# A four-batch sequence block on one core: statistics and four pairs pinned in VectorE's order, 14 instead of 12 pairs of a causal convolution made ahead

## The chip, the cores and the metric

The kernel runs on one core of a Trainium2 chip. Five engines work side by side, each through its own queue in order: TensorE (PE; its weight loads are shown apart as PEld), VectorE (DVE), ScalarE (ACT), GpSimd (POOL) and SyncE (SP). An instruction that waits for something holds up all that stands behind it in its queue. SP and POOL also issue the DMA transfers, which run on 16 DMA engines. Matrix products go to PSUM, everything else lies in SBUF or in device memory. The metric is the device time of one execution in microseconds.

## The reference

The input is `x` of shape (4, 512, 128, 64): 4 batches, 512 time steps, and 128 x 64 = 8192 channels D. All is float32. Layer 0 is, for each batch:

```python
xn = layernorm(x)                       # over the 8192 channels
k, v, r = xn @ Wk, xn @ Wv, sigmoid(xn @ Wr)          # to 64 states
s_t = decay * s_(t-1) + k_t * v_t       # a scan over time
x = x + (r * s) @ Wo
x = x + gelu(conv(layernorm(x), freq_W) + freq_b)     # 3 taps along 128, 64 to 64 channels
to = causal_depthwise_conv(layernorm(x), time_W) + time_b   # 3 taps along time, per channel
x = x + layernorm(to)
x = x + gelu(x @ ffn_W1 + ffn_b1) @ ffn_W2 + ffn_b2   # 64 to 256 to 64
```

Layer 1 splits the result into a moving average of 25 steps and the rest; the rest goes through a Fourier transform in time, a product with complex weights for 128 modes and the transform back; the sum of both is the output.

## The kernel before

In layer 0 channels lie on partitions and the 512 time steps along the free axis. The 8192 channels make 64 chunks of 128 and 32 pairs of chunks; a pair's tile is 128 x 1024 (512 KB). Batches b = 0 to 3 pass through six stages:

- `project` (J, L321): for each pair it loads weights, `xt` (channels on partitions) and a slice `xk` of `x` with time on partitions (L349, 512 KB). `bn_stats` (L353) takes mean and variance of two slices of 512 channels of `xk` into `stt`; the weights are scaled (L366) and multiplied (L369). For b above 1 the tile `xk` comes from the tags `sq` and `x2` in turn, with two buffers each.
- `scan` (Z, L380): `bn_aggr` over all of `stt` (L388), rows of mean and scale spread over the partitions (L240, L284), and then a chain of small steps between TensorE and VectorE (L430 to L469) with the scan over time (L449).
- `attend_and_convolve` (A, L475): per pair, `attend` (L491, then on VectorE L493 and L497) and `convolve` (L512 to L529). Sums over all channels (L250) give the next mean and variance; `x2` goes to device memory (L530).
- `convolve_time` (C, L598): per pair, `normed` loads `x2` and normalizes it on VectorE (L565, L568); `tapped` makes the causal convolution, the first tap on ScalarE (L573), the others on VectorE (four instructions of L577), a small correction on GpSimd (L583), and stores the result `to` (L584). The squares (L623) and the sums (L250) follow.
- `open_feed` (O) and `feed_forward` (F, L665): for each chunk `widen` (L674, then L678 on ScalarE), `narrow` (L685 into the only buffer of `pa`, which L690 on VectorE empties into `x4t`) and `store` (L699, L706 or L708, L710). The residual of the pair two ahead is made by L642, L643, L651 and L654.

`in_turn` (L744) runs two stages of different batches beside each other, by weights that the stages yield: C of batch b beside A of b + 1, and then F of b beside J and Z of b + 2. TensorE's instructions keep the order in which the program traces them. On the other engines a scheduler chooses the order: it goes by a model of durations and takes an instruction early when the model says that its inputs and buffers are there. `tc.keep_in_program_order(i)` adds one edge for it: `i` must stand behind the instruction that was traced just before it on its engine. The edge adds no wait at run time.

While F runs for b = 0 and 1, `convolve_ahead` (L586) makes the first `AHEAD` pairs of the causal convolution of b + 1, in the tiles `x1` and `z`. F advances it once in each odd chunk after chunk 8: two advances for the rows, then two for each pair (`normed`, and `tapped`). These instructions are pinned already. C of that batch then starts at pair `AHEAD`, and reads the `to` of the pairs made ahead back from device memory for their squares and sums (L628 to L631), spread over its own pairs. Layer 1 (L798) follows after all of layer 0.

Of the kernel before, what the change touches and what calls it, by code (L numbers as in the profile page):

```python
# [79 lines left out]
def layer0(ctx, tc, dram, x, xt, vecs, wkvr, wo, wdec, wconv, fbias, w1, fb1, w2, fb2, x4):  # L80
# [72 lines left out]
    tb_all = const.tile([P, NCH], F32, name="tb_all")  # L153
    fix = const.tile([P, NCH, 2], F32, name="fix")

    AHEAD = 12
    halves = [slice(0, H), slice(H, P)]

    def neighbours(q, c):
# [161 lines left out]
    def project(b):  # L321
        pa = two(ps_m, "m") if b == 1 else two(ps_a, "a")
        held[0] = b == 1
        if b == 0:
            psum_w = ps_p.tile([P, SL], F32, tag="p", name="psum_w")
        stt = rowp.tile([P, NT, NS, 6], F32, tag="stt", name="stt")
        for i in range(NPR):
            first, last = i == 0, i == NPR - 1
            if unscanned[0]:

                wq, xk = two(fr, "x1")[:, :, 0 : 4 * S + 3], spare("z", SL)
            elif b == 1:

                both = spare("wx", 4 * S + SL)
                wq, xk = both[:, :, 0 : 4 * S], both[:, :, 4 * S :]
            else:

                xk = two(bk, "sq" if i % 2 else "x2")
                if i % 2 == 0:
                    pairs = spare("wx", 4 * S + SL).rearrange("p k n -> p (k n)")[:, 0 : 16 * S]  # L340
                    pairs = pairs.rearrange("p (c s) -> p c s", c=4)
                    nc.sync.dma_start(pairs, wkvr[2 * i : 2 * i + 4, :, 0 : 4 * S].rearrange("c p s -> p c s"))
                wq = pairs[:, i % 2 * 2 : i % 2 * 2 + 2, :]
            if b < 2:
                n = 4 * S + 2 * (b == 0)
                nc.sync.dma_start(wq[:, :, 0 : n], wkvr[2 * i : 2 * i + 2, :, 0 : n].rearrange("c p s -> p c s"))
            xp = load_x(b, i)
            s, h = i // 2, i % 2 * 2
            nc.sync.dma_start(  # L349
                xk, x[b, h * P : (h + 2) * P, s * SL : (s + 1) * SL].rearrange("(t p) d -> p t d", p=P)  # L350
            )
            for t in range(2):
                nc.vector.bn_stats(stt[:, h + t, s, :], xk[:, t, :])  # L353
            if b == 0:
                nc.gpsimd.memset(wq[:, :, n:], 1.0)
                for j in range(2):
                    c = 2 * i + j

                    w = wq[:, j, :]
                    nc.tensor.matmul(  # L360
                        psum_w[0 : S + 2, 0 : 4 * S + 3], lhsT=w[:, 3 * S : 4 * S + 2], rhs=w,
                        start=c == 0, stop=c == NCH - 1,
                    )
            for j in range(2):
                w = wq[:, j, 0 : 3 * S]
                nc.vector.tensor_scalar_mul(w, w, vec[:, G1, 2 * i + j : 2 * i + j + 1])  # L366
            for j in range(2):
                for k in range(2):
                    nc.tensor.matmul(  # L369
                        pa[:, k, :], lhsT=wq[:, j, k * P : (k + 1) * P], rhs=xp[:, j, :],  # L370
                        start=first and j == 0, stop=last and j == 1,
                    )
                yield 1.0
        kvrg = rowp.tile([P, 2, SL], F32, tag="kvrg", name="kvrg")
        nc.scalar.copy(kvrg, pa)
        held[0] = False
        projected[b] = (kvrg, stt, psum_w) if b == 0 else (kvrg, stt)
# [220 lines left out]
    def convolve_time(b):  # L598
        bank = of_a if b == B - 1 else of_p
        made = AHEAD if b in ahead else 0  # L600
        moment = carried.pop(b)
        if made:
            rb, mb = ahead.pop(b)
        else:
            rb, mb = yield from rows(bank, *moment, "rm" if b == B - 1 else "rm3")
        st = bank()
        waiting, added = [], 0
        n = NPR - made
        for k in range(n + 2):
            while waiting and waiting[0][0] == k - 2:  # L610
                add_up(st, 0, *waiting.pop(0)[1:], added == 0, added == NPR - 1)
                added += 1
            if k < n:
                if b == B - 1:

                    x2, xr, to, sq = spare("xp", SL), spare("x1", SL), spare("z", SL), two(bk, "sq")
                else:
                    x2 = bk.tile([P, 2, SL], F32, tag="kx", name="x2", bufs=3)
                    xr, to = two(bk, "kd"), bk.tile([P, 2, SL], F32, tag="k3", name="to", bufs=3)
                    sq = bk.tile([P, 2, SL], F32, tag="sq4", name="sq4", bufs=2)  # L620
                normed(b, made + k, x2, xr, rb, mb)
                tapped(b, made + k, xr, to)
                nc.scalar.activation(sq, to, AF.Square)  # L623
                waiting.append((k, to, sq))
                i = k * made // n
                if i != (k + 1) * made // n:

                    to = fetch("kh", tod, b, i)  # L628
                    sq = bk.tile([P, 2, SL], F32, tag="mid", name="sq5", bufs=4)
                    nc.scalar.activation(sq, to, AF.Square)  # L630
                    waiting.append((k, to, sq))  # L631
            yield 7.0 * (NPR + 2) / (n + 2)
        mean, sq = yield from finish(st, bank, 4)
        causal[b] = moments(mean, sq, 4)
# [30 lines left out]
    def feed_forward(b):  # L665
        x3s = opened.pop(b)
        mids, x4s, obs = {}, {}, {}

        def widen(c, m):
            x3 = x3s[c // 2][:, c % 2, :]  # L670
            pm = c_bank() if m else two(ps_m, "m")
            for h in range(2):
                hs = slice(h * H, (h + 1) * H)
                nc.tensor.matmul(  # L674
                    pm[:, h, :], lhsT=w1_sb[hs, m * P : (m + 1) * P], rhs=x3[hs, :], start=True, stop=True
                )
            mid = mids[c, m] = bk.tile([P, 2, SL], F32, tag="mid", name="mid", bufs=4)
            nc.scalar.activation(mid, pm, AF.Gelu_apprx_tanh, bias=fb1_sb[:, m : m + 1])  # L678

        def narrow(c):  # L680
            pa = ps_p.tile([P, SL], F32, tag="p", name="pa")
            for m in range(2):
                mid = mids.pop((c, m))
                for h in range(2):
                    nc.tensor.matmul(  # L685
                        pa[h * H : (h + 1) * H, :], lhsT=w2_sb[:, m, :], rhs=mid[:, h, :],
                        start=(m == 0), stop=(m == 1),
                    )
            x4t = x4s[c] = bk.tile([P, SL], F32, tag="x4t", name="x4t", bufs=3)
            nc.vector.scalar_tensor_tensor(x4t, pa, fb2_sb, x3s[c // 2][:, c % 2, :], ALU.add, ALU.add)  # L690
            if c % 2:
                x3s.pop(c // 2)

        def store(c):
            x4t = x4s.pop(c)
            pool, tag = (ps_s, "s") if free_s[0] else (ps_p, "p")
            pt = pool.tile([P, NT, P], F32, tag=tag, name="pt")
            for t in range(NT):
                nc.tensor.transpose(pt[:, t, :], x4t[:, t * P : (t + 1) * P], ident)  # L699
            s = c // 4  # L700
            if c % 4 == 0:
                obs[s] = bk.tile([P, NT, SL], F32, tag="ob", name="ob")
            o = obs[s][:, :, c % 4 * P : (c % 4 + 1) * P]
            if c // 2 % 2:
                for h in range(2):
                    nc.scalar.copy(o[:, :, halves[1 - h]], pt[:, :, halves[h]])  # L706
            else:
                nc.scalar.copy(o, pt)  # L708
            if c % 4 == 3:
                nc.gpsimd.dma_start(  # L710
                    x4[b][:, s * SL : (s + 1) * SL].rearrange("(t p) d -> p t d", p=P), obs.pop(s)
                )

        early = None
        for c in range(NCH + 2):
            if c < NCH:
                widen(c, 0)
                widen(c, 1)
            i = c // 2 + 2
            if i < NPR:  # L720
                if c % 2:
                    x3s[i] = add_residual(b, i, *coming)
                else:
                    coming = residual(b, i)
            if 0 < c <= NCH:
                narrow(c - 1)
            if c > 1:
                store(c - 2)
            if b + 2 < B and c > 8 and c % 2:
                early = early or convolve_ahead(b + 1)  # L730
                next(early, None)
            yield 4.5
# [360 lines left out]
```

## Time and profile before

| quantity | value |
|---|---|
| three runs | 3827.88, 3835.29 and 3841.98 us, median 3835.29 |
| the profiled execution | 3840.34 us; span 3838.6 us; mean granted TensorE clock 0.978 |
| TensorE, VectorE, ScalarE, GpSimd busy | 3630.4, 2687.1, 1761.3, 507.6 us |
| F of batch 0 beside J and Z of batch 2 | about 825 to 1255 us |
| C of batch 1 beside A of batch 2 | about 1255 to 1480 us |
| F of batch 1 beside J and Z of batch 3 | about 1515 to 1935 us |
| C of batch 2 beside A of batch 3 | about 1935 to 2165 us |
| layer 1 | from about 2840 us |
| `bn_stats`, mean of one | 684 ns |
| L565, L568, mean of one (128 x 1024) | 1220 ns |
| L577, mean of one | 744 ns |

A group line of the profile has the line of the kernel, engine, operation, tiles and shapes, the count, the busy time and the mean of one, then the idle time of the engine just before and what ended it. Successive VectorE instructions overlap a little, so that they start closer together than their durations. A line of waits has who waited for whom, the total in us, how often, and the longest.

### The profile page before, as it was taken

Reading aid. Unit: us, or ns where it says so; the run is one execution under the profiler, and the core shown is the slowest. Engines: PE = TensorE matmul, PEld = TensorE weight load, DVE = VectorE, ACT = ScalarE, POOL = GpSimd, SP = SyncE. Lnnn points to the kernel's source line nnn. Section 1 sums busy time; section 2 is a strip of 40 time slices with the busy share of each in tenths; the row PEclk is TensorE's granted clock in tenths of the full one; section 3 lists DMA queues with packets and bytes.
Section 4 is the critical chain, followed back from the end, with each engine's and each line's share of the span. In section 5 each row is a group of like instructions: output and inputs, shape, how many; then the busy total and the mean of one; then the engine's idle time right before and its main releaser. Section 6 shows DMA issues by size and latency. Waiting matters only on the chain. (4 is left out here: it accounts for less than half of the span.)

```text
span 3838.6 us, 44851 instructions
## 1 busy us (share of the span) xinstructions
PE 3630.4 (95%) x15945; PEld 1345.7 (35%) x15945; DVE 2687.1 (70%) x3498; ACT 1761.3 (46%) x2491; POOL 507.6 (13%) x782
## 2 busy tenths in 40 slices
PE   9999999988999999899999988999989999999999
PEld 4433322233333223333322322333322743327533
DVE  4445659986667796766789799855558267892577
ACT  0022346644666465456656578867744210142100
POOL 0000012210111121011122121100013100121001
PEclk9999989999999999999999999999999999999999
DMA  9867647787665688866568677645558368994687
GB/s 312 267 204 247 224 157 256 262 308 263 234 227 187 228 274 278 286 232 238 199 235 275 210 255 253 211 162 178 182 196 285 130 216 287 307 308 159 197 294 267
DMA packets 428087, 910.71 MB, mean 237 GB/s; under 512 B 33176, under 2 KB 83544, under 8 KB 423768
## 3 DMA queue, kind: packets, MB, share of 16 engines
q1 hardware_dynamic: 349568, 634.55, 49.1%
q0 software_dynamic: 75776, 271.62, 20.3%
q8 instruction: 127, 2.08, 0.2%
q10 hardware_dynamic: 2520, 1.67, 0.1%
q14 instruction: 96, 0.79, 0.1%
HBM read 639.21 MB, written 268.50 MB: 236 GB/s over the span
## 5 line engine op out<-in xcount | busy, mean ns | idle before, releaser
L685 PE MATMUL pa<-mid,w_sb 128*64 128x512 f32 x2048 | 501.1, 610 | 57.7 <-DVE x4t L690 57.1
L678 ACT ACTIVATE mid<-m,fb_sb 128x1024 f32<-128x1024 f32 x256 | 284.8, 1112 | 283.6 <-PE m L674 283.4
L690 DVE SCALAR_TENSOR_TENSOR x4t<-pa,fb_sb,x 128x512 f32<-128x512 f32 x252 | 187.9, 746 | 307.0 <-PE pa L685 307.0
L674 PE MATMUL m<-x,w_sb 64*128 64x512 f32 x1008 | 289.8, 647 | 0.0
L678 ACT ACTIVATE mid<-c,fb_sb 128x1024 f32<-128x1024 f32 x256 | 283.0, 1105 | 1.7 <-PE c L674 1.6
L685 PEld LDWEIGHTS pa<-mid,w_sb 128*64 128x64 f32 x2048 | 125.3, 136 | 402.0 <-issue 246.0
L674 PE MATMUL c<-x,w_sb 64*128 64x512 f32 x1008 | 263.5, 596 | 1.3 <-ACT mid L678 1.3
L369 PE MATMUL a<-xp,wx 128*128 128x512 f32 x512 | 245.8, 607 | 0.5 <-DVE me L267 0.5
L961 PE MATMUL b<-xin,avg_sb 128*128 128x512 f32 x512 | 230.8, 593 | 3.3 <-DVE xin L967 3.3
L938 ACT COPY two<-a 128x512 f32<-128x512 f32 x64 | 37.5, 585 | 427.2 <-PE a L933 427.2
L967 DVE TENSOR_TENSOR xin<-b,pm 128x512 f32<-128x512 f32 x256 | 159.0, 683 | 97.0 <-PE b L964 82.0
L532 ACT ACTIVATE sq<-x 128x1024 f32<-128x1024 f32 x128 | 134.9, 1054 | 198.3 <-DVE x L529 198.2
L577 DVE SCALAR_TENSOR_TENSOR to<-kd,vec,to 128x510 f32<-128x510 f32 (+1 forms) x288 | 210.5, 744 | 16.2 <-ACT to L573 14.5
L651 ACT ACTIVATE kd<-kd,vec 128x512 f32<-128x512 f32 x256 | 193.3, 809 | 3.4 <-DVE kd L643 3.4
L843 DVE COPY xf<-b 128x256 f32<-128x256 f32 x128 | 54.3, 424 | 189.2 <-PE b L907 188.6
L250 PE MATMUL st<-x,ones 128*32 128x512 f32 x512 | 172.6, 605 | 13.9 <-DVE x L529 13.7
L491 PE MATMUL a<-rst,wo_sb 64*128 64x512 f32 x512 | 151.6, 666 | 32.7 <-DVE x L493 30.4
L699 PEld LDWEIGHTS pt<-ident,x4t 128*128 128x128 f32 x1024 | 108.1, 141 | 209.4 <-ACT mid L678 145.2
L864 DVE TENSOR_TENSOR uv<-xin 128x1024 f32<-128x1024 f32 x128 | 155.5, 1226 | 33.9 <-DMA edge<-x 14.4
L493 DVE TENSOR_TENSOR x<-a,xp 128x1024 f32<-128x1024 f32 x128 | 156.1, 1220 | 23.3 <-PE a L491 19.9
L699 PE MATMUL pt<-ident,x4t 128*128 128x128 f32 x1024 | 169.3, 288 | 1.5 <-ACT ob L706 1.5
L530 POOL DMA_DIRECT2D x<-x x128 | 93.3, 729 | 575.8 <-DVE x L529 545.8
(241 smaller groups left out, 6572.0 us busy)
## 6 DMA issues: line engine op xcount, KB each, us to landing
xp<-in_xt SPq DMA_DIRECT2D x256, 512.0 KB
xin<-x SPq DMA_DIRECT2D x128, 1024.0 KB
kh<-to SPq DMA_DIRECT2D x152, 512.0 KB
x<-x POOLq DMA_DIRECT2D x128, 512.0 KB, 3.9
kx<-x SPq DMA_DIRECT2D x128, 512.0 KB
x<-ob POOLq DMA_DIRECT2D x64, 1024.0 KB, 6.5
out<-xin POOLq DMA_DIRECT2D x64, 1024.0 KB, 6.9
x<-x SPq DMA_DIRECT2D x96, 512.0 KB
```

Source lines behind the costliest of these rows:

```text
L250: nc.tensor.matmul(st[32 * q : 32 * q + 32, :], lhsT=ones, rhs=src[:, j, :], start=first, stop=last,)
L369: nc.tensor.matmul(pa[:, k, :], lhsT=wq[:, j, k * P : (k + 1) * P], rhs=xp[:, j, :], start=first and j == 0, stop=last and j == 1,)
L493: nc.vector.tensor_tensor(x1, at, xp, ALU.add)
L577: tap = nc.vector.scalar_tensor_tensor(to[:, j, k:], xr[:, j, : SL - k], vec[:, w, c], to[:, j, k:], ALU.mult, ALU.add)
L651: tc.keep_in_program_order(nc.scalar.activation(d[:, j, :], d[:, j, :], AF.Identity, bias=vec[:, B4, c], scale=vec[:, G4, c]))
L674: nc.tensor.matmul(pm[:, h, :], lhsT=w1_sb[hs, m * P : (m + 1) * P], rhs=x3[hs, :], start=True, stop=True)
L678: nc.scalar.activation(mid, pm, AF.Gelu_apprx_tanh, bias=fb1_sb[:, m : m + 1])
L685: nc.tensor.matmul(pa[h * H : (h + 1) * H, :], lhsT=w2_sb[:, m, :], rhs=mid[:, h, :], start=(m == 0), stop=(m == 1),)
L690: nc.vector.scalar_tensor_tensor(x4t, pa, fb2_sb, x3s[c // 2][:, c % 2, :], ALU.add, ALU.add)
L699: nc.tensor.transpose(pt[:, t, :], x4t[:, t * P : (t + 1) * P], ident)
L961: nc.tensor.matmul(po[j], lhsT=avg_sb[:, j, :], rhs=xin[:, j, :], start=True, stop=False)
L967: nc.vector.tensor_tensor(by_n(xin[:, j, :]), by_n(po[j]), by_c(pm[j % 2][:, j // 2, :]), ALU.add)
```

## The change

The first statistics instruction of each pair of the projections of batches 2 and 3 is kept in program order on VectorE. In the causal stage of a batch that had pairs made ahead (batches 1 and 2), the first `normed` instruction of its first four own pairs is kept in program order too. 14 pairs instead of 12 are made ahead, and the advances begin after chunk 4 instead of chunk 8.

```diff
-    AHEAD = 12
+    AHEAD = 14
...
             for t in range(2):
-                nc.vector.bn_stats(stt[:, h + t, s, :], xk[:, t, :])
+                stats = nc.vector.bn_stats(stt[:, h + t, s, :], xk[:, t, :])
+                if b > 1 and t == 0:
+
+                    tc.keep_in_program_order(stats)
...
-                normed(b, made + k, x2, xr, rb, mb)
+
+                normed(b, made + k, x2, xr, rb, mb, made > 0 and k < 4)
                 tapped(b, made + k, xr, to)
...
-            if b + 2 < B and c > 8 and c % 2:
+            if b + 2 < B and c > 4 and c % 2:
                 early = early or convolve_ahead(b + 1)
                 next(early, None)
```

`normed` has the argument `pinned` already: with it the first of its two VectorE instructions is passed to `tc.keep_in_program_order`.

## The prediction

> **What bounds the kernel now.** First the page's busy shares:
>
> ```profile
> PE 3630.4 (95%) x15945; PEld 1345.7 (35%) x15945; DVE 2687.1 (70%) x3498; ACT 1761.3 (46%) x2491; POOL 507.6 (13%) x782
> ```
>
> Then stretches of the span, because the limits differ by stage (busy time of PE, PEld, DVE, ACT, POOL, then granted clock, DMA share, GB/s):
>
> ```profile
> 832.00:864.00 32.00, 31.14 (x113) 11.23 (x112) 26.74 (x39) 18.09 (x21) 0.00 (x0) 1.00 0.98 344
> 864.00:896.00 32.00, 27.46 (x103) 10.08 (x103) 24.94 (x38) 14.39 (x20) 0.84 (x1) 0.95 1.00 348
> 896.00:928.00 32.00, 25.41 (x99) 10.69 (x97) 22.63 (x37) 12.58 (x17) 2.02 (x3) 0.89 0.65 228
> ...
> 928.00:1184.00 256.00, 253.22 (x999) 93.15 (x998) 158.70 (x199) 154.05 (x209) 25.54 (x30) 1.00 0.64 226
> ```
>
> TensorE is the bound, but not everywhere. From 928 to 1184 (feed-forward of batch 0 beside the projection of batch 2) it works 253 of 256 us at full clock with DVE at 62%. In the 96 us before, the same stage loses TensorE time and clock while DMA is full. 1536 to 1632 repeats that for batch 3. The waits of TensorE in 832:928 and then in 1536:1632, and DVE's order at one place:
>
> ```profile
> PE pa L685 <- DVE x4t L690: 6.6, 6, 2.5
> PE p L240 <- DVE x4t L690: 5.4, 2, 5.2
> ...
> PE p L240 <- DVE x4t L690: 8.3, 2, 6.8
> PE pa L685 <- DVE x4t L690: 7.1, 5, 2.5
> ```
>
> ```profile
> 868.19 0.73 DVE L690 SCALAR_TENSOR_TENSOR x4t<-pa,fb_sb,x 128x512 f32<-128x512 f32 x1
> 872.09 1.29 DVE L353 BATCH_NORM_STATS2 stt<-x 128x6 f32<-128x512 f32 x2 [3.17 <-DMA x<-in_x]
> 873.42 1.29 DVE L353 BATCH_NORM_STATS2 stt<-sq 128x6 f32<-128x512 f32 x2
> 875.61 1.29 DVE L353 BATCH_NORM_STATS2 stt<-x 128x6 f32<-128x512 f32 x2 [0.90 <-DMA x<-in_x]
> 876.82 0.73 DVE L690 SCALAR_TENSOR_TENSOR x4t<-pa,fb_sb,x 128x512 f32<-128x512 f32 x1
> ```
>
> The reader sees x4t, which frees the single bank `pa`, queued behind statistics that wait for their own loads. All 64 statistics of batch 2 run from 811 to 912, although the matmuls of the same projection go on to 1184.
>
> The second place is the end of a feed-forward, where the scan of the next batch runs (TensorE, 1200 to 1262):
>
> ```profile
> 1228.60 1.96 PE L456 MATMUL a<-rst,qo 64*64 64x512 f32 x2 [5.41 <-DVE rst L451]
> 1230.49 2.08 PE L674 MATMUL m<-x,w_sb 64*128 64x512 f32 x4
> ...
> 1256.12 1.48 PE L491 MATMUL a<-rst,wo_sb 64*128 64x512 f32 x4 [2.09 <-DVE x L493]
> 1260.18 2.08 PE L491 MATMUL a<-rst,wo_sb 64*128 64x512 f32 x4 [2.58 <-DVE x L493]
> ```
>
> Just before, DVE has the next causal stage's own pairs (L565 `kd<-x` at 1211.81, 1223.64, 1235.05) in between the scan's steps.
>
> **The change, term by term.** A pin is an edge in the scheduler's graph only: it adds no semaphore, it fixes that the instruction stands behind the DVE instruction traced just before it.
>
> *Statistics pinned (batches 2 and 3).* 64 of the 128 statistics (t = 0) get the edge. The other 64 are free, but a slot is released only after both, so at most four pairs (two tags, two buffers) are loaded ahead; the burst cannot form. No work is removed: 128 x 0.684 us on DVE, and 32 loads of 512 KB per batch, are spread over some 400 us. What the burst cost: undisturbed, groups of L685 start 6.09 us apart (1106.72, 1112.81). From 843.07 to 900.03 lie eight steps, 56.96 against 48.7 us: 8.2 lost. The next step holds one group for the rows (eight matmuls, 0.95 us): 14.50 against 7.04, 7.5 lost. For batch 3: 1525.34 to 1582.98 is 57.64, 8.9 lost; the next step 16.85, 9.8 lost. Together 34.4 us. It cannot return whole, since a later rows group without statistics near it (1609.89) still waits 1.4 us. Bounds -34 and -10 (DMA stays the limit in part); I take **-28**, nearer to the undisturbed rows.
>
> A rule of the Trainium skill speaks against this part (DMA: Bandwidth & Descriptors, Rules for kernel authors): issue a DMA early and wait for it late. By it paced loads would show a latency for every pair, the third rival's sum; the rows show early loads at a share of 1.00 with statistics still waiting for them, so I go by the rows.
>
> *What the paced statistics meet.* By the order of TensorE's groups, a pair's projection starts after an even chunk in batch 2, so its statistics follow that chunk's x4t. Behind such x4t DVE idles, in turn, 1.36 and 5.34 us (before the x4t at 1121.05 and 1108.71): 1.37 us of two statistics fits. The free half goes wherever the scheduler thinks the load has landed. In batch 2 one chunk in four has no slack: x4t at 1118.27 ends 0.06 us before TensorE's group at 1119.07, behind a 1.45 us wait for `wx` from DMA. 13 such places x 1.37 = 18 us at most; batch 3 mostly has 1.5 us or more there. Traffic in this stretch rises from 226 GB/s by 16.8 MB over 400 us, 42 GB/s, under the 348 seen. Bounds 0 and +18; **+5**.
>
> *14 pairs ahead.* Two pairs for each of batches 1 and 2 leave the causal stage for the feed-forward before it. By start-to-start times a pair occupies DVE for 2 x 1.13 + 4 x 0.66 = 4.9 us, ACT for 2 x 0.81, POOL for an add (0.93) and a DMA issue (0.73), with a 512 KB load and store. In the feed-forward this lies beside TensorE (DVE 62% busy, ACT 60%): nothing; if that cover went, 9.8 us a batch. The advances run from chunk 5 instead of 9 and need 30 of 31 odd chunks, so the last taps come at chunk 63 instead of 59. New are two refetches of `to` per batch, 0.36 us on SP's queue each and 2.1 MB in all, hidden at a DMA share of 0.8; the square (1.05) and the sums are there either way. **0**.
>
> *First four own pairs pinned.* They leave the scan's neighbourhood: four pairs less five taps, 16 us of DVE between 1211 and 1255, and as much from 1894 to 1935. TensorE's waits on DVE there are 1.03 + 1.16 + 0.37 + 5.41 + 0.94 + 2.09 + 2.58 = 13.6, and 3.23 + 2.60 + 2.27 = 8.1 at the second place. The granted clock is 0.89 and 0.79 in 1216:1280 and 0.95 and 0.84 in 1888:1952, 10.2 + 6.7 us of clock. The start-up latency of attention stays, so of 38.6 I take under a third, **-12**; bounds 0 and -28.
>
> The skill's rule (TensorE: Matmul & The Clock Gate, HAM oscillation) is that the clock falls to half after idle gaps above some 3.4 us. The row at 1260.18 shows 2.08 us for a group that took 1.13, with no gap above 2.6 within 25 us before it. By the rule, as an estimate, only the 5.41 gap costs clock, about 1.7 us instead of 16.9, and this term would be -7.
>
> *The causal stage itself* (1254 to 1478). DVE had there 32 x 3.4 (attention) + 20 x 4.9 - 16 made early = 190 us; now 32 x 3.4 + 18 x 4.9 = 197, in 225. DVE is 93% busy from 1312 to 1472, TensorE 98%. The cost is 0 to +13 for both stages if DVE becomes the bound, a gain of 6 if its idle start-up is filled; **+4**.
>
> *The scan's start.* Its aggregates were ready at 914; now they follow the last pair (chunk 52 or 53): aggregates 1.9, small ones 0.6, POOL 1.3. TensorE has two half pairs and two chunks (12.2 us) before it needs them, DVE about 12 of work. 0 to +6; **+2**.
>
> SP's queue keeps its loads in order, and one for `xk` now waits there for a pinned statistic: behind it stand kx, kh, xp, wx. With two buffers per tag that is about 24 us of lead; nothing.
>
> Sum: -28 + 5 + 0 - 12 + 4 + 2 = -29 us. The profiled execution took 3840.3 (span 3838.6 and 1.7 around it), 5.0 above the median of the three runs; from the median, 3835.3 - 29 = **3806 us**, -0.75%.
>
> **Rivals.**
> - *The starts are bound by DMA anyway.* For: share 0.98 to 1.00 and 344 to 348 GB/s. Against: it is the burst itself that fills it, 226 GB/s after. Only 10 come back: -10 + 5 - 12 + 4 + 2 = -11, 3824.
> - *Everything returns:* -34 - 28 - 6, 3767. Against: start-up latencies.
> - *Slower: paced statistics hold x4t up all through the projection.* Each would wait as statistics do now (36.2 us over 22 waits, 1.65) and run 1.37, 3.0 us ahead of x4t. For: in-order DVE, and the free half scheduled by a modelled landing. Against: usual slack 3.35. At 13 tight places 39 us, in batch 3 at every other pair 13 x 1.5 = 20: -28 + 59 - 12 + 4 + 2 = +25, 3860. It turns the sign from about 0.6 us lost per pair (34 us over 54 pairs).
> - *The pin does not hold the order:* if the instruction traced before is itself early, statistics float as now; only the tail's -12 + 4 remains, 3827. Against: that instruction is mostly x4t, which waits for TensorE.
>
> **How the numbers follow.** Forecast 0.62 (its own range 3788 to 3828), DMA-bound starts 0.14, everything 0.08, slower 0.10, no hold 0.06. 0.5% (19 us) is about what a measurement can tell. Below 3816: four fifths of the forecast, 0.50, all of "everything", a little of DMA-bound: 0.60. Above 3854: most of the slower rival and a little else, 0.10. Same: 0.30. The range leaves out half of "everything" and most of the slower rival: 3776 to 3848.
>
> **What would show it.** L353 for batches 2 and 3 spread over about 350 us each, 832:896 below a DMA share of 0.9, TensorE's waits for x4t in 832:928 and 1536:1632 under 5 us each (right); waits for x4t between 928 and 1184 above 15 us where now 2.3 (the slower rival); L565 `kd<-x` absent before the scan's last step, the 5.41 wait gone. A causal stage over 230 us, or statistics still in a burst, would make the forecast wrong.

## The result, and the profile after

Twenty runs of the changed kernel have a median of 3827.28 us (3817.85 to 3835.73), beside 3834.32 us for twenty runs of the kernel before on the same chip: a ratio of 0.9989 with a 95% interval of [0.9979, 1.0]. The change is worth 7 us or nothing, where 29 us were forecast. Behind L353 the lines of the changed kernel are numbered 3 higher, and 4 higher from the call of `normed` in `convolve_time` on: L369, L494 and L568 were L366, L491 and L565; L678, L689 and L694 were L674, L685 and L690.

The busy shares say little:

```profile
PE 3620.5 (95%) x15945; PEld 1342.4 (35%) x15945; DVE 2683.1 (70%) x3498; ACT 1763.0 (46%) x2491; POOL 512.9 (13%) x782
```

The stretches that were shown of before (busy time of PE, PEld, DVE, ACT, POOL, granted clock, DMA share, GB/s):

```profile
832.00:864.00 32.00, 31.57 (x118) 11.21 (x118) 22.78 (x31) 17.44 (x21) 0.00 (x0) 1.00 0.79 278
864.00:896.00 32.00, 26.86 (x108) 11.59 (x106) 13.47 (x18) 13.69 (x20) 0.84 (x1) 0.95 0.54 181
896.00:928.00 32.00, 31.68 (x126) 11.40 (x122) 18.93 (x26) 19.77 (x27) 3.30 (x4) 1.00 0.71 241
928.00:1184.00 256.00, 234.00 (x908) 84.25 (x910) 174.76 (x231) 141.63 (x190) 23.99 (x28) 1.00 0.71 245
```

The burst is gone: from 832 to 896 DMA is at 0.79 and 0.54, where it was at 0.98 and 1.00, and from 832 to 928 TensorE works 90 of 96 us, where it worked 84. But from 928 to 1184, where it worked 253 of 256 us, it now works 234. The waits of TensorE in that last stretch add up to those 22 us (6.2 us of them for ScalarE; before, 2.3 us for x4t were the only ones):

```profile
PE pa L689 <- DVE x4t L694: 15.7, 17, 2.0
PE c L678 <- ACT mid L682: 6.2, 9, 0.7
```

So the wait for x4t has moved from the start of the stage into its middle. The statistics of batch 2 in the whole stage (800 to 1260) show what VectorE does instead; count, shortest, median and longest duration in ns, first and last start, and below them VectorE's idle time in front of them:

```profile
L353 DVE BATCH_NORM_STATS2 stt<-x x32: 676/692/696, 806.6 to 1177.4; 128x6 f32<-128x512 f32 x32
L353 DVE BATCH_NORM_STATS2 stt<-sq x32: 676/688/695, 807.9 to 1187.8; 128x6 f32<-128x512 f32 x32
...
  DMA sq<-in_x: 64.2, 12
  DMA x<-in_x: 42.0, 16
```

The same view of the kernel before:

```profile
L353 DVE BATCH_NORM_STATS2 stt<-x x32: 675/683/695, 811.0 to 908.7; 128x6 f32<-128x512 f32 x32
L353 DVE BATCH_NORM_STATS2 stt<-sq x32: 673/685/694, 812.3 to 912.2; 128x6 f32<-128x512 f32 x32
...
  DMA x<-in_x: 14.6, 8
  DMA sq<-in_x: 3.0, 3
```

Before, these 64 instructions had waited 14.6 + 3.0 us for their loads. Spread over 381 us, they wait 106.2 us, at 28 places. The sequence of VectorE at one of them:

```profile
947.60 0.74 DVE L694 SCALAR_TENSOR_TENSOR x4t<-pa,fb_sb,x 128x512 f32<-128x512 f32 x1
948.26 0.68 DVE L353 BATCH_NORM_STATS2 stt<-sq 128x6 f32<-128x512 f32 x1
955.02 0.69 DVE L353 BATCH_NORM_STATS2 stt<-sq 128x6 f32<-128x512 f32 x1 [6.08 <-DMA sq<-in_x]
955.63 0.73 DVE L694 SCALAR_TENSOR_TENSOR x4t<-pa,fb_sb,x 128x512 f32<-128x512 f32 x1
```

Then SyncE's queue, which issues the loads, and TensorE's next group of matmuls into `pa`:

```profile
948.97 0.37 SPq L349 DMA_DIRECT2D sq<-in_x  x1
```

```profile
956.42 1.94 PE L689 MATMUL pa<-mid,w_sb 128*64 128x512 f32 x8 [1.28 <-DVE x4t L694]
```

The first `sq` statistic is pinned (t = 0 of a pair). It is the last reader of its tile, because the free t = 1 of that pair ran long ago. When it ends at 948.94, SyncE issues the next load into that tile at 948.97. The second `sq` statistic is the free t = 1 that reads this load, four pairs further on; the scheduler put it directly behind. VectorE stands for 6.08 us, the length of the load, x4t stands behind it, and TensorE's next group waits 1.28 us for that. The two statistics can't be halves of one pair: one load brings both halves, so the second would have had nothing to wait for. The other places are alike. At 12 of the 28 the statistic that waits stands directly behind one of its own tag, and its load was issued 0.03 us after the end of that one; at ten more only two or three scalings (L369) stand between.

**Where the time is.** Four parts per feed-forward, from the starts of L674 and L491 (by their numbers in the kernel before) in the traces: *start*, the first ten chunks; *middle*, chunk 10 to 54; *end*, chunk 54 to the first matmul of the next attention; *causal*, from there to the next feed-forward. Each is the sum over batches 0 and 1, in us of the profiled execution. The kernels named e1 to e12 (there is no e7) follow below.

| kernel | start | middle | end | causal | sum | span |
|---|---|---|---|---|---|---|
| before | 153.5 | 544.4 | 132.3 | 517.7 | 1347.9 | 3838.6 |
| after | 134.4 | 566.4 | 124.0 | 520.2 | 1344.9 | 3829.3 |
| e1: after, both statistics pinned | 125.4 | 542.1 | 125.0 | 518.3 | 1310.8 | 3796.7 |
| e2: after, no statistic pinned | 150.2 | 545.2 | 125.3 | 518.7 | 1339.4 | 3824.8 |
| e3: before, t = 0 pinned | 128.8 | 577.0 | 133.9 | 515.7 | 1355.5 | 3841.4 |
| e4: before, both statistics pinned | 122.8 | 548.8 | 132.6 | 517.3 | 1321.4 | 3799.5 |
| e5: e4 and the four own pairs | 123.0 | 547.5 | 121.8 | 529.8 | 1322.0 | 3811.5 |
| e6: e4 and 14 ahead | 126.0 | 542.2 | 138.6 | 498.6 | 1305.4 | 3789.2 |
| e8: e1, weight scalings pinned | 137.8 | 701.8 | 120.7 | 529.6 | 1489.9 | 3987.6 |
| e9: after, pin on t = 1 instead | 152.4 | 545.0 | 125.7 | 524.4 | 1347.5 | 3821.4 |
| e10: e6 with 15 ahead | 124.9 | 541.5 | 137.7 | 501.1 | 1305.2 | 3788.8 |
| e11: before, 14 ahead alone | 149.0 | 543.8 | 137.4 | 499.9 | 1330.1 | 3811.6 |
| e12: before, four own pairs alone | 151.3 | 546.6 | 123.8 | 530.7 | 1352.4 | 3838.8 |

From before to after: starts -19.1, middles +22.0 (21.4 of it in batch 0, 0.6 in batch 1), ends -8.4, causal stages +2.5: together -3.0. The other 6.3 us between the two spans lie where nothing was edited: 4.5 before the end of batch 1's attention, a point which the thirteen profiles reach between 767.0 and 777.9 us, and 1.9 in layer 1.

The end of the feed-forward, TensorE and then VectorE:

```profile
1235.63 1.53 PE L459 MATMUL a<-rst,qo 64*64 64x512 f32 x2 [3.37 <-DVE rst L454]
...
1260.83 1.13 PE L494 MATMUL a<-rst,wo_sb 64*128 64x512 f32 x4 [1.55 <-DVE x L496]
1265.74 2.08 PE L494 MATMUL a<-rst,wo_sb 64*128 64x512 f32 x4 [3.78 <-DVE x L496]
```

```profile
1256.71 1.22 DVE L568 TENSOR_TENSOR kd<-x,rm 128x1024 f32<-128x1024 f32 x1
```

The first own pair (`kd<-x`) now starts at 1256.71, after the scan; the 5.41 us wait has become 3.37.

### The profile page after: what moved, and what is told of

It reads as the page before. It is cut to its first block, busy times and chain, and to the rows that moved or that the text cites. A ratio compares the mean times of both kernels' runs of the same rounds, so it can differ in the third digit from the quotient of the medians.

```text
span 3829.3 us, 44885 instructions
## 1 busy us (share of the span) xinstructions
PE 3620.5 (95%) x15945; PEld 1342.4 (35%) x15945; DVE 2683.1 (70%) x3498; ACT 1763.0 (46%) x2491; POOL 512.9 (13%) x782
## 3 DMA queue, kind: packets, MB, share of 16 engines
q8 instruction: 127, 2.08, 0.2%
## 5 line engine op out<-in xcount | busy, mean ns | idle before, releaser
L689 PE MATMUL pa<-mid,w_sb 128*64 128x512 f32 x2048 | 499.7, 609 | 55.5 <-DVE x4t L694 55.3
L694 DVE SCALAR_TENSOR_TENSOR x4t<-pa,fb_sb,x 128x512 f32<-128x512 f32 x252 | 187.7, 745 | 225.6 <-PE pa L689 225.6
L678 PE MATMUL m<-x,w_sb 64*128 64x512 f32 x1008 | 289.4, 647 | 0.8 <-ACT mid L682 0.4
L678 PE MATMUL c<-x,w_sb 64*128 64x512 f32 x1008 | 263.7, 596 | 9.8 <-ACT mid L682 9.8
L689 PEld LDWEIGHTS pa<-mid,w_sb 128*64 128x64 f32 x2048 | 124.9, 136 | 398.9 <-issue 216.5
L372 PE MATMUL a<-xp,wx 128*128 128x512 f32 x512 | 244.9, 605 | 0.5 <-DVE me L267 0.5
L580 DVE SCALAR_TENSOR_TENSOR to<-kd,vec,to 128x510 f32<-128x510 f32 (+1 forms) x272 | 198.2, 748 | 15.1 <-ACT to L576 11.0
L494 PE MATMUL a<-rst,wo_sb 64*128 64x512 f32 x512 | 151.8, 667 | 29.5 <-DVE x L496 26.8
L580 DVE SCALAR_TENSOR_TENSOR z<-x,vec,z 128x511 f32<-128x511 f32 x240 | 175.9, 746 | 5.3 <-ACT z L576 2.3
```

Of the source, the lines that this page charges most:

```text
L372: nc.tensor.matmul(pa[:, k, :], lhsT=wq[:, j, k * P : (k + 1) * P], rhs=xp[:, j, :], start=first and j == 0, stop=last and j == 1,)
L580: tap = nc.vector.scalar_tensor_tensor(to[:, j, k:], xr[:, j, : SL - k], vec[:, w, c], to[:, j, k:], ALU.mult, ALU.add)
L678: nc.tensor.matmul(pm[:, h, :], lhsT=w1_sb[hs, m * P : (m + 1) * P], rhs=x3[hs, :], start=True, stop=True)
L689: nc.tensor.matmul(pa[h * H : (h + 1) * H, :], lhsT=w2_sb[:, m, :], rhs=mid[:, h, :], start=(m == 0), stop=(m == 1),)
```

## The experiments

Two theories for the 22 us. **U, the unpinned half:** only t = 0 was pinned, and the free t = 1 is placed where its load has just been issued; pin both, and the loss goes. **P, the pacing:** statistics spread along the feed-forward cost that much by themselves, because VectorE, in order, must take them and their loads among the x4t; pin both, and the loss stays or grows.

**e1. Both halves pinned, with all of the change.**

```diff
-                if b > 1 and t == 0:
+                if b > 1:
```

> The changed kernel, with both statistics of a pair pinned instead of the first one only. Theory U (the free second statistic): in the changed kernel it stands directly behind the pinned one that frees its buffer, and so waits on VectorE for a load that was issued 0.05 us before; pinned, it waits for a load that is four pairs old. Then VectorE's waits for statistics from 800 to 1260 us fall from 106 us to under 30, the matmuls of feed-forward 0 from chunk 10 to chunk 54 take 273 to 278 us instead of 294.2 (272.8 before the change), and the time is 3805 to 3815. Rival P (the pacing itself: 44 us more VectorE work and 42 GB/s more traffic in this stretch make x4t late): 290 us or more for these chunks and 3822 to 3832.

Measured: 3798.07 us (3792.74 to 3803.36), ratio to before 0.9897 [0.9879, 0.9915]. The middles are back at 542.1 us. The time is 7 us below the range that U gave; U had named no gain at the starts, and they are 9.0 us better than after's. The statistics of batch 2, idle time in front of them:

```profile
L353 DVE BATCH_NORM_STATS2 stt<-sq x32: 674/680/695, 807.2 to 1158.7; 128x6 f32<-128x512 f32 x32
L353 DVE BATCH_NORM_STATS2 stt<-x x32: 675/682/694, 808.4 to 1148.4; 128x6 f32<-128x512 f32 x32
...
  DMA sq<-in_x: 3.0, 1
  DMA x<-in_x: 1.3, 1
```

The wait of TensorE from 928 to 1184, and that stretch:

```profile
PE pa L689 <- DVE x4t L694: 1.6, 3, 1.2
```

```profile
928.00:1184.00 256.00, 254.38 (x1018) 94.70 (x1020) 190.81 (x252) 157.65 (x214) 28.57 (x34) 1.00 0.76 263
```

The statistics are as widely spread as in the changed kernel, VectorE does more work in the stretch (190.81 us against 174.76, since the stage gets further in it), DMA moves more, and TensorE is back at 254 of 256 us. With one more pin, 106.2 us of waits on VectorE became 4.3: from the sixth pair of a tag on, a load is 46 to 52 us old when its statistics run. P falls.

**e2. The change without any pinned statistic.**

```diff
-                if b > 1 and t == 0:
-
-                    tc.keep_in_program_order(stats)
```

> The changed kernel without any pin on the statistics (14 pairs ahead and the four pinned pairs stay). Both theories: the burst of statistics is back, so feed-forward 0 and 1 take some 75 and 78 us again from their first chunk to chunk 10 (67.8 and 66.6 in the changed kernel), and chunk 10 to 54 takes 272 to 276 us. What remains is the end of the feed-forward, -8 us, and the causal stage, +3: 3825 to 3832. A time below 3820 would mean that the statistics' pin is a loss on balance, above 3836 that the other two parts are.

Measured: 3824.74 us (3816.35 to 3828.59), ratio 0.9969 [0.9955, 0.9983]. The starts are back at 150.2 and the middles at 545.2. The half pin as the change made it therefore bought nothing: with it the ratio to before was 0.9989, without it 0.9969.

**e3. The kernel before, with the half pin alone.**

```diff
-                nc.vector.bn_stats(stt[:, h + t, s, :], xk[:, t, :])
+                stats = nc.vector.bn_stats(stt[:, h + t, s, :], xk[:, t, :])
+                if b > 1 and t == 0:
+                    tc.keep_in_program_order(stats)
```

> The kernel before with only the pin on the first statistic of a pair, as the change has it; 12 pairs ahead, no pinned pairs. Theory U and P alike: the first ten chunks gain 19 us for both batches, chunks 10 to 54 of feed-forward 0 lose about 21: 3832 to 3840. If the loss of 21 us came from 14 pairs ahead or from the earlier start of the advances, the time would be 3812 to 3818.

Measured: 3842.3 us (3832.66 to 3852.08), ratio 1.0019 [1.0004, 1.0034]. Starts -24.7, middles +32.6: the half pin by itself makes the kernel 0.2% slower, just clear of its interval, and it does so without the other parts of the change. Starts and middles both moved by more than the -19 and +21 expected, and the time is 2 us above the range; 6.1 us of the middles lie in batch 1 here.

**e4. The kernel before, with both halves pinned and nothing else.** As e3, with `if b > 1:`.

> The kernel before with both statistics of a pair pinned and nothing else. Theory U: -19 at the starts and 0 to +5 in between, 3816 to 3822. Rival P: 3832 to 3840.

Measured: 3807.32 us (3801.26 to 3813.12), ratio 0.9922 [0.9904, 0.9939]. Starts -30.7, middles +4.4. This was better than U had expected, because the starts return more when no free half is left to load early in them (30.7 us of the 34.4 that the prediction had counted).

**e9. The pin on the other half.**

```diff
-                if b > 1 and t == 0:
+                if b > 1 and t == 1:
```

> The changed kernel with its pin on the statistic of the second half of a pair (t = 1) instead of the first. The instruction traced just ahead of it, t = 0, is free, and so is nothing that the pin holds. If the pin only holds an instruction as far as the free half ahead of it is held, the burst is back (all statistics of batch 2 between 800 and 930 us), the middle of the first feed-forward takes 272 to 276 us, and the whole 3820 to 3830 us. If one pinned half of any kind paces the loads, and the other then waits for them: 290 us or more there, and 3825 us or more in all.

Measured: 3823.67 us (3814.82 to 3842.5), ratio 0.9982 [0.9967, 0.9997]. The statistics of batch 2:

```profile
L353 DVE BATCH_NORM_STATS2 stt<-x x32: 675/685/695, 804.2 to 903.5; 128x6 f32<-128x512 f32 x32
L353 DVE BATCH_NORM_STATS2 stt<-sq x32: 634/682/695, 805.5 to 905.6; 128x6 f32<-128x512 f32 x32
```

The burst is back, between 804 and 906, with starts of 152.4 us. The pin on t = 1 only says "behind t = 0", which is free and early. The pin on t = 0 says "behind whatever was traced before it on VectorE", and that is late. The edge is no better than the instruction that it points to; so to pin both is to make a chain with a late first link.

**e8. Pinned scalings.** In e1 VectorE still waited for `wx`, at an unpinned scaling: 4.4 us once in the scan, 1.4 us at 950.80. So the same remedy was tried there.

```diff
-                nc.vector.tensor_scalar_mul(w, w, vec[:, G1, 2 * i + j : 2 * i + j + 1])
+                scaled = nc.vector.tensor_scalar_mul(w, w, vec[:, G1, 2 * i + j : 2 * i + j + 1])
+                if b > 1:
+                    tc.keep_in_program_order(scaled)
```

> Both statistics pinned, with the whole change, and the scalings of the projection's weights pinned as well in the batches after the first two. If an unpinned instruction that waits for its own load is what costs, the 4.1 us wait for wx in the scan at 1216 goes, and the 11 us of such waits between 928 and 1184, of which TensorE sees a part: 3788 to 3798 us. If pinned scalings come too late for the projection's matmuls, TensorE waits there instead: 3800 to 3815 us.

Measured: 3985.85 us (3974.03 to 3990.01), ratio 1.0393 [1.0371, 1.0416]. The second theory had the direction, and was far off in size. (L374, L691 and L696 are here what L372, L689 and L694 are in the changed kernel.) All of TensorE's waits, and the largest of VectorE's, from 896 to 1256:

```profile
PE a L374 <- DVE wx L369: 58.6, 23, 3.5
```

```profile
DVE x4t L696 <- PE pa L691: 154.1, 34, 8.6
```

One turn of it, VectorE and then TensorE:

```profile
1010.69 0.74 DVE L696 SCALAR_TENSOR_TENSOR x4t<-pa,fb_sb,x 128x512 f32<-128x512 f32 x1
1011.35 1.28 DVE L353 BATCH_NORM_STATS2 stt<-x 128x6 f32<-128x512 f32 x2
1012.55 0.53 DVE L369 TENSOR_SCALAR wx<-wx,vec 128x192 f32<-128x192 f32 x2
1020.38 0.75 DVE L696 SCALAR_TENSOR_TENSOR x4t<-pa,fb_sb,x 128x512 f32<-128x512 f32 x1 [7.31 <-PE pa L691]
```

```profile
1012.90 3.65 PE L374 MATMUL a<-xp,wx 128*128 128x512 f32 x4 [3.50 <-DVE wx L369]
...
1020.76 1.88 PE L374 MATMUL a<-xp,wx 128*128 128x512 f32 x4
```

The pin puts the scaling behind the statistics and these behind x4t, and x4t needs TensorE's last group. TensorE's matmul of the projection (L374) waits for the scaling, and the next `pa`, for which the next x4t waits, stands behind L374 in TensorE's order. Each engine waits in turn for the other, and the group after the 3.5 us gap also runs at half rate (3.65 against 1.88 us). A statistic can be pinned late because nobody needs it before the scan; a scaling can't.

**e5, e6, e11, e12. The pairs.** The two other parts of the change, each with both statistics pinned (e5: four own pairs pinned, 12 ahead; e6: 14 ahead, no own pair pinned) and each on the kernel before (e11: 14 ahead; e12: four own pairs). The edit of e6 against e1 and of e5 against e1:

```diff
-                normed(b, made + k, x2, xr, rb, mb, made > 0 and k < 4)
+                normed(b, made + k, x2, xr, rb, mb)
```

```diff
-    AHEAD = 14
+    AHEAD = 12
...
-            if b + 2 < B and c > 4 and c % 2:
+            if b + 2 < B and c > 8 and c % 2:
```

> Both statistics pinned and the four own pairs pinned, but 12 pairs ahead, made from chunk 8 on as in the kernel before. It splits what the two other parts of the change do to the ends of the feed-forwards (last chunks up to the scan) and the causal stages: with both statistics alone the ends took 67.7 and 64.8 us and the causal stages 266.8 and 250.5; with everything 63.0 and 62.0, and 263.4 and 254.8. If the four pinned pairs free the scan: ends of 62 to 64 us, and causal stages of about 268 and 257 us or longer, since two pairs more are made in them: 3797 to 3808 us. If having 14 pairs done earlier frees it: the ends stay at 65 to 68 us.

> Both statistics pinned, 14 pairs ahead from chunk 4 on, no pinned pairs. If it is the pinned pairs that free the scan: ends of 66 to 69 us, causal stages of about 262 and 248 us, 3795 to 3806 us in all. If the 14 pairs are the cause: ends of 62 to 64 us.

> The kernel before with the 14 pairs ahead from chunk 5 on, and nothing else of the change. If the pairs are worth what they were with both statistics pinned (causal stages 12 and 7 us shorter, ends 4 and 2 us longer): 3820 to 3828 us. If the burst of free statistics in the first ten chunks leaves no room for an earlier start: the starts grow by what the causal stages save, 3830 to 3838 us.

> The kernel before with the first four own pairs of a causal stage pinned, and nothing else of the change. If they do what they did with both statistics pinned: ends of the feed-forwards 5 us shorter each, causal stages 3 and 10 us longer, 3834 to 3842 us in all. As predicted blind, the pinned pairs take 12 us off: 3819 to 3827 us.

| kernel | median us | ratio to before |
|---|---|---|
| e5 | 3811.60 (3808.03 to 3815.96) | 0.9945 [0.9929, 0.9960] |
| e6 | 3789.84 (3784.56 to 3790.99) | 0.9884 [0.9866, 0.9902] |
| e11 | 3815.03 (3807.88 to 3823.38) | 0.9965 [0.9951, 0.9979] |
| e12 | 3837.48 (3828.10 to 3843.84) | 1.0018 [1.0007, 1.0029] |

The ends: 63 and 59 us with pinned own pairs (e5), 72 and 67 without (e6). So it is these pins that free the scan. But the causal stages after them become longer by more. e12 against before: ends -8.5, causal +13.0. e11 against before: ends +5.1, causal -17.8. The own pairs on VectorE in e11, unpinned, whose attention begins at 1249.18 on TensorE:

```profile
1204.13 1.21 DVE L565 TENSOR_TENSOR kd<-x,rm 128x1024 f32<-128x1024 f32 x1
...
1215.95 1.22 DVE L565 TENSOR_TENSOR kd<-x,rm 128x1024 f32<-128x1024 f32 x1
...
1227.36 1.23 DVE L565 TENSOR_TENSOR kd<-x,rm 128x1024 f32<-128x1024 f32 x1
```

and in e2, which is e11 with the pins, whose attention begins at 1240.71:

```profile
1239.27 1.22 DVE L565 TENSOR_TENSOR kd<-x,rm 128x1024 f32<-128x1024 f32 x1
```

Unpinned, own pairs start 45 us before the attention; pinned, 1.4 us before it. VectorE's work in the scan was not a loss but work of the next stage, done early. Pinned, it is done later, in a stage where VectorE has little room: from e11 to e2 the ends become 12.1 us shorter and the causal stages 18.8 us longer. e12 came out as e5 had let expect, and not as predicted blind. e11 and e6 were some 5 us faster than expected; e5 was 4 us slower than its range, with 994 us in layer 1, where nothing was edited, against 989 in the kernel before.

**e10. One more pair ahead, to go on from e6.**

```diff
-    AHEAD = 14
+    AHEAD = 15
...
-            if b + 2 < B and c > 4 and c % 2:
+            if b + 2 < B and c > 0 and c % 2:
```

> Both statistics pinned, no pinned pairs, 15 pairs ahead from chunk 1 on instead of 14 from chunk 5 on. With 12 and with 14 pairs the two causal stages together took 517.3 and 498.6 us, and the ends of the feed-forwards 132.6 and 138.6 us. If a pair costs what it takes out of the causal stages less what it adds at the ends: causal stages of about 489 us, ends of about 141 us, and 3782 to 3790 us in all. If the feed-forwards have no room left for a pair: the middles and ends grow by 10 us or more, and 3790 to 3800 us.

Measured: 3792.57 us (3770.84 to 3801.19), ratio 0.9901 [0.9878, 0.9923], which overlaps e6. Neither expectation holds: the time lies in the range of the second, but the middles and ends did not grow, and the causal stages did not shrink (501.1 against 498.6). What bounds a causal stage once 14 pairs are gone was not settled. e6 stays the best: both statistics pinned, 14 pairs ahead, no own pair pinned.

## Why the prediction was wrong

**What bounds the kernel: right.** The burst fills DMA (for the first 64 of the 96 us that the prediction named; after that its share was 0.65) and holds x4t; that is where the starts lose. With both halves pinned 30.7 of the 34.4 us counted there came back (e4).

**Statistics pinned, -28: mechanism right, size partly.** After: -19.1; e3, the pin alone: -24.7. The claim beside it, that at most four pairs are loaded ahead and the burst can't form with one half pinned, held: L353 spread over 381 us and DMA at 0.79 and 0.54 in 832:896. TensorE's waits for x4t in 832:928 are 5.1 (rows) and 0.7 us, where 12.0 stood.

**What the paced statistics meet, +5 within 0 and +18: here the prediction failed.** It measured +22.0, above the upper bound (+32.6 in e3). The text had seen that the free half "goes wherever the scheduler thinks the load has landed", and then priced it at its 1.37 us of running time at tight places. What the free half costs is its load: 106.2 us over 28 places is 3.8 us each, and x4t is behind it. The step left out was to ask what releases that load. It is the pinned half of four pairs earlier, and the scheduler put the free half directly behind the release. Batch 3 (beside the feed-forward of batch 1) lost 0.6 us in the middle, but only 18.4 us of such waits lie there, against 81.1 us for batch 2; so the runs don't show whether batch 3 also had more slack, as the prediction says.

**14 pairs ahead, 0: wrong, to the good.** e11 measures -17.8 over the stages, and 0.35% (13 us) by its ratio. The prediction asked whether the added work in the feed-forward was hidden (it was in the middles, 543.8 against 544.4; the ends grew by 5.1), and put the relief of the causal stage into a sum with the work that the pins push into it.

**First four own pairs pinned, -12, and the causal stage, +4: wrong together.** The ends moved by -8.5 (e12), within the size given. The causal stages moved by +13.0 (with 12 pairs ahead), the upper bound, so the part is +4.5 instead of -8. The waits for VectorE in the scan were read as loss, without asking what the work in front of them spared later. In the changed kernel the shorter causal stages of the 14 pairs hide this: +2.5 there is the sum of two parts that e11 and e12 show as -17.8 and +13.0, and of 7.3 us that come of the parts together.

**The scan's start, +2: 0.** No wait for the aggregates is among TensorE's waits from 1184 to 1260, which are 3.4, 1.7 and 0.2 us.

**The sum.** The single parts give +7.5 (e3), -17.8 (e11) and +4.5 (e12), -5.8 together; the change gave -3.0 over the same stages. The result lies inside the range given, 21 us from the forecast. Of the rivals, "slower" had the right mechanism (waits for x4t between 928 and 1184 above 15 us: 15.7) and the wrong size: of the 81.1 us of waits for batch 2 in the middle VectorE's slack took some 60, and for batch 3 almost nothing was lost there. "DMA-bound starts" would have given nearly this time for a wrong reason.

**The two rules that were weighed.** The rule of the Trainium skill to issue a DMA early and wait late ("DMA: Bandwidth & Descriptors", Rules for kernel authors) was set aside in favour of the rows. It describes the failure exactly: the load at 948.97 was waited for from 948.94 on. It doesn't speak against pacing, though: in e1 the loads are as late in the stage and cost 4.3 us, since four pairs lie between a load and its statistics.

For the clock, the Trainium skill's page "TensorE: Matmul & The Clock Gate" (HAM oscillation) would, by the prediction's estimate, have put the scan's part at -7 instead of -12; the ends gave -8.4. Its threshold of some 3.4 us of idle is not what the rows show: in the kernel before a group of four that takes 1.13 us elsewhere took 2.08 us after 2.58 us of idle. The granted clock was 0.50 there from 1256.8 to 1270.4, and no gap in the 25 us ahead of that was above 2.1 us. Nor does the gap just in front decide alone: after 1.55 us the group took 1.13 us in the changed kernel and 1.91 us in e2.

## What to carry to other kernels

When one of several readers of a buffer is held in order, look at the others: a free reader may be placed directly behind the release of its own buffer, and then waits there for a whole load, in front of all that follows on its engine. Pin all readers of a buffer or none, and see that the first link of the chain hangs on something late; pin only what nobody needs soon (in e8 two engines waited for each other in turn). Before taking work off a crowded place, ask where it would be done instead: pairs made ahead in the feed-forward paid (-17.8 us), own pairs pushed out of the scan came back in the next stage (+13.0 for -8.5).

## What the runs showed of the hardware

- Loads of the same size took unequally long: the 512 KB load issued at 948.97 released its reader at 955.02, 6.05 us later; that of `x`, issued at 937.26, at 941.49, 4.2 us later. Three other loads of 512 KB had been issued in the 4.3 us before the former, and none in the 4.0 us before the latter. It goes on so: from 921 to 1144 a statistic that waits for `sq` starts 5.5 to 7.4 us after the issue of its load, one that waits for `x` 3.4 to 4.2 us. That the other loads are the cause is argued, not shown.
- A pin on an instruction as short as 0.3 us (the scaling) cost some 190 us in all: e8 against e1 by spans is 190.9 us, of which 159.7 lie in the middles of the two feed-forwards.
- Twelve of the thirteen kernels, all but e8, have the same order of VectorE's instructions up to the end of batch 1's attention, and yet reach it up to 9.8 us apart (768.1 to 777.9 us). So a difference of a few us is better read from the stages than from two spans.
